# Token gathers of a recommendation kernel: two rows a buffer, a fill after each gather, adds three groups later

## The chip, the cores and the metric

The kernel runs on one core of one Trainium2 chip. The metric is the device time of one execution in microseconds (us), as the median of several executions without a profiler. Before the change it is 5566.13 us, the median of three runs (5557.75, 5566.13 and 5580.29). The engines are named as in the profile: PE is the matrix engine and PEld its weight loads, DVE the vector engine, ACT the scalar engine, POOL the GpSimd engine, SP the sync engine.

## The reference

For 16384 samples, a wide-and-deep recommendation model. Each sample has 32 token indices into a table of 50000 rows of 300 floats, three lists of 20 indices into small tables (1000, 5000 and 10000 rows of 64), and four single indices into tables of 20 to 1000 rows. All is float32.

```python
tok = word_emb[token_idx].mean(axis=1)          # 32 rows of 300 floats
e1 = emb_mh1[mh1_idx].mean(axis=1)              # 20 rows of 64; e2, e3 alike
o1 = emb_oh1[oh1_idx]                           # one row of 64; o2, o3, o4 alike
emb = jnp.concatenate([tok, e1, e2, e3, o1, o2, o3, o4], axis=1)   # 748 wide
...
```

On `emb` follow three layers with bias and relu (748 to 1024 to 512 to 256) and a last one to a single number. A "wide" sum of one weight per small-table index is added to it, and a sigmoid gives the output.

## The kernel before

The 16384 samples are cut into 128 tiles of 128 samples, one sample to a partition; four tiles make a block of 512 samples, on which the three layers run.

The token rows [...] are gathered from HBM: one indirect DMA on POOL (line 188) fetches one row of 300 floats for each of the 128 partitions. A tile needs 32 of them, the whole kernel 4096. The generator `tokens` (line 180) makes them in groups of `TOK_GROUP` = 4 into one buffer of the pool `tokp` (line 81, three buffers), at a pitch of 320 floats after 32 floats of margin. DVE then adds the four rows: two and two at once (line 196, 600 elements), then the two halves (line 204), then into the tile's row `g` (line 205); the first group of a tile adds the halves straight into `g` (line 202). A gather into a buffer must wait until DVE has added up what the buffer held three groups before, and each gather also waits for the gather eight before it to have landed, since eight semaphores take turns.

The small tables are not gathered. For each sample a count of how often each row is used is made by one-hot vectors: `one_hots` (line 252) compares indices with an iota on DVE (line 260), `counts` (line 268) multiplies the one-hots on PE (line 278) and ACT writes the counts to SBUF as 8-bit floats (line 285). `small_sums` (line 293) multiplies the counts with the tables on PE (line 303), and DVE folds the result into `g` (line 310). `transposed` (line 338) turns four finished `g` on PE (line 345) and DVE scales them (line 346); `mlp` (line 365) runs the layers (line 353 on PE, line 362 on ACT).

The order on each engine is the order in which the program is written (`manual_schedule`, line 411). A loop over 128 tiles holds a loop of `STEPS` = 11 steps. In each step the program writes, in this order: the one-hots of the next step, the counts of this step, the due share of `tokens` of this tile, the due share of `small_sums` of the tile before, and the due share of `mlp` of the block before. `Paced` (line 387) decides what is due: in step i it asks for more until done * 11 >= size * i. So DVE meets, in order, the compares of a step, then any token adds of that step, then the compares of the next; an add that waits for a gather holds the compares behind it.

```python
it, ix = load_indices(0)
...
            toks = Paced(tokens(g, it[:, s, :].bitcast(U32)), N_TOK // TOK_GROUP, STEPS)
        for i in range(STEPS):
...
                counts(cnt, hot_now, i)
                toks.go()
```

Of the kernel before, what the change touches and what calls it, by code (L numbers as in the profile page):

```python
# [8 lines left out]
F32 = mybir.dt.float32  # L9
# [8 lines left out]
P = 128  # L18
N_TOK, TOK_D = 32, 300
N_MH, EMB = 20, 64  # L20
ROW = EMB + 1
D1, D2, D3 = 1024, 512, 256
TOK_GROUP = 4
TOK_PITCH = 320
BLOCK = 512
HALF = P // 2
N_SMALL = 3 * N_MH + 4
# [17 lines left out]
def kernel(  # L45
# [21 lines left out]
    nc = tc.nc  # L67
# [7 lines left out]
    for f in SMALL:  # L75
        n = -(-tables[f].shape[0] // P)
# [1 line left out]
        n_h += n  # L78
    PER_BANK = 512 // n_h

    tokp = ctx.enter_context(tc.tile_pool(name="tok", bufs=3))
    const = ctx.enter_context(tc.tile_pool(name="const", bufs=1))
    idxp = ctx.enter_context(tc.tile_pool(name="idx", bufs=2))
    keyp = ctx.enter_context(tc.tile_pool(name="keys", bufs=1))
# [40 lines left out]
    first = const.tile([P, 2, N_SMALL], I32, name="first")  # L125
# [10 lines left out]
    for part0 in range(0, n_h, PART):  # L136
        raw = cp.tile([P, PART, ROW], F32, name="raw", tag="counts")
        for f in SMALL:
            table, (h0, h1) = tables[f], slices[f]
            full, rest = divmod(table.shape[0], P)  # L140
            a, b = max(h0, part0), min(h0 + full, part0 + PART)
            if a < b:
                nc.sync.dma_start(
                    out=raw[:, a - part0 : b - part0, :],
# [5 lines left out]
        for a in range(0, PART, 23):  # L150
            b = min(a + 23, PART)
# [25 lines left out]
    bd_sb = const.tile([1, 1], F32, name="bd_sb")  # L177
    nc.scalar.dma_start(out=bd_sb, in_=bd)

    def tokens(g, it):  # L180

        for q in range(N_TOK // TOK_GROUP):

            space = tokp.tile([P, TOK_GROUP * TOK_PITCH + 64], F32, name="tok_rows")
            rows = space[:, 32 : 32 + TOK_GROUP * TOK_PITCH].rearrange("p (t d) -> p t d", d=TOK_PITCH)
            for t in range(TOK_GROUP):
                j = q * TOK_GROUP + t
                nc.gpsimd.indirect_dma_start(  # L188
                    out=rows[:, t, 0:TOK_D],
                    out_offset=None,  # L190
                    in_=word,
                    in_offset=bass.IndirectOffsetOnAxis(ap=it[:, j : j + 1], axis=0),
                )
            n = TOK_GROUP // 2
            while n > 1:
                nc.vector.tensor_add(  # L196
                    rows[:, 0:n, 0:TOK_D], rows[:, 0:n, 0:TOK_D], rows[:, n : 2 * n, 0:TOK_D]
                )
                n //= 2
            first, second = rows[:, 0, 0:TOK_D], rows[:, 1, 0:TOK_D]  # L200
            if q == 0:
                nc.vector.tensor_add(g[:, 0:TOK_D], first, second)
            else:
                nc.vector.tensor_add(first, first, second)  # L204
                nc.vector.tensor_add(g[:, 0:TOK_D], g[:, 0:TOK_D], first)  # L205
            yield 1

    def load_indices(blk):


        b0 = blk * BLOCK
        it = idxp.tile([P, NSUB, N_TOK], I32, name="it")
        nc.sync.dma_start(
            out=it, in_=idx[b0 : b0 + BLOCK, 0:N_TOK].rearrange("(s p) c -> p s c", p=P)
        )
        ix = keyp.tile([P, NSUB // 2, 2, N_SMALL], I32, name="ix")
        for s in range(NSUB):
            nc.sync.dma_start(
                out=ix[(s % 2) * HALF : (s % 2 + 1) * HALF, s // 2],
                in_=idx[b0 + s * P : b0 + (s + 1) * P, IDX_MH:IDX_COLS].rearrange(  # L220
                    "(f p) c -> p f c", p=HALF
                ),
            )
        return it, ix

    def lookup_keys(ix):

        pairs = NSUB // 2
        low = keyp.tile([P, pairs, 2, N_SMALL], I32, name="low")
        nc.vector.tensor_single_scalar(low, ix, P - 1, op=ALU.bitwise_and)
        nc.vector.tensor_single_scalar(ix, ix, 7, op=ALU.logical_shift_right)
        keys = keyp.tile([P, pairs, 2, 2 * N_SMALL], BF16, name="keys")
        for r in range(pairs):
            view = keys[:, r].rearrange("p w (f c) -> p w f c", f=2)
            nc.vector.tensor_copy(view[:, 0], low[:, r])  # L238
            nc.vector.tensor_add(view[:, 1], ix[:, r], first)
        pk = ps_h.tile([P, pairs, 2, P], BF16, name="pk", tag="ph")  # L240
        for r in range(pairs):
            for w in range(2):
                nc.tensor.transpose(pk[:, r, w, :], keys[:, r, w, :], ident_bf)  # L243
        sc = scp.tile([P, pairs, 2, 2, HALF, 2], BF16, name="sc")
        n = pairs * 2 * P
        nc.vector.tensor_copy(
            sc.rearrange("p r w t b d -> p (r w t b) d"),
            pk.rearrange("p r w b -> p (r w b)").unsqueeze(2).to_broadcast([P, n, 2]),
        )
        return sc  # L250

    def one_hots(sc, s, i):

        b = i * ONEHOT
        rows = min(ONEHOT, HALF - b)
        row1 = ohp.tile([P, ONEHOT, P], BF16, name="row1")
        slice1 = ohp.tile([P, ONEHOT, n_h], BF16, name="slice1")
        for w, (one, n) in enumerate(((row1, P), (slice1, n_h))):
            shape = [P, rows, n // 2, 2]
            nc.vector.tensor_tensor(  # L260
                one[:, 0:rows, :].rearrange("p i (n d) -> p i n d", d=2),
                iota[:, 0:n].rearrange("p (n d) -> p n d", d=2).unsqueeze(1).to_broadcast(shape),
                sc[:, s // 2, w, s % 2, b : b + rows, :].unsqueeze(2).to_broadcast(shape),
                ALU.is_equal,
            )
        return row1, slice1
# [26 lines left out]
    def small_sums(g, cnt):  # L293


        by_slice = cnt.rearrange("l f p h -> l (f p) h")
        for i in (0, 2, 6, 4):
            pair = SMALL[i : i + 2]
            pg = ps_g.tile([P, 2, 3 * ROW], F32, name="pg")
            for j, f in enumerate(pair):  # L300
                h0, h1 = slices[f]
                for h in range(h0, h1):
                    nc.tensor.matmul(  # L303
                        pg[:, j, :], by_slice[:, :, h], terms[:, h, :], start=(h == h0), stop=(h == h1 - 1)
                    )
                    if h < h1 - 1:
                        yield 1
            at = TOK_D + i * ROW
            n = len(pair)
            nc.vector.tensor_reduce(  # L310
                g[:, at : at + n * ROW].rearrange("p (f d) -> p f d", f=n),
                pg[:, 0:n, :].rearrange("p f (c d) -> p f d c", c=3),
                AX.X,
                ALU.add,
            )
            yield n if i != 6 else n + LULL

    def wide_term(g):
        wide = wp.tile([P, 1], F32, name="wide")
        at = TOK_D + EMB  # L320
        nc.vector.tensor_reduce(
            wide,
            g[:, at : at + 6 * ROW].rearrange("p (c d) -> p c d", d=2 * ROW)[:, :, 0:2],
            AX.XY,
            ALU.add,
        )
        nc.vector.tensor_add(wide, wide, g[:, G_COLS - 1 : G_COLS])
        return wide
# [87 lines left out]
    for t in range(tiles + 1):  # L416
        s = t % NSUB
        sums = None
        if before:
            sums = Paced(small_sums(*before), n_h + LULL, STEPS)  # L420
        if t < tiles:
            if s == 0 and t:
                it, sc = next_it, next_sc
            g = gp.tile([P, G_COLS], F32, name="g")
            cnt = cp.tile([P, 2, HALF, n_h], FP8, name="cnt", tag="counts")
            toks = Paced(tokens(g, it[:, s, :].bitcast(U32)), N_TOK // TOK_GROUP, STEPS)
        for i in range(STEPS):
            if t < tiles:
                hot_now = hot
                if s == 1 and i == 0 and t + NSUB < tiles:  # L430
                    next_it, ix = load_indices(t // NSUB + 1)
                if s == 2 and i == 0 and t + NSUB < tiles + 1:
                    next_sc = lookup_keys(ix)
                if i < STEPS - 1:
                    hot = one_hots(sc, s, i + 1)
                elif t + 1 < tiles:
                    hot = one_hots(next_sc if s == NSUB - 1 else sc, (s + 1) % NSUB, 0)
                counts(cnt, hot_now, i)
                toks.go()
            if sums:  # L440
                sums.go()
            if layers:
                layers.go()
        if before:
            sums.finish()
            gs.append(before[0])
            wides.append(wide_term(before[0]))
        before = (g, cnt) if t < tiles else None
        if len(gs) == NSUB:
            if layers:  # L450
                layers.finish()
            layers = Paced(mlp(t // NSUB - 1, transposed(gs), wides), mlp_size, NSUB * STEPS)
            gs, wides = [], []
# [40 lines left out]
```

## Time and profile before

| what | value |
|---|---|
| median of three runs | 5566.13 us |
| the profiled execution's own time | 7340.1 us |
| its span from first to last instruction | 7338.3 us |
| busy: PE, DVE, ACT, POOL | 5808.1, 3542.7, 2657.3, 4082.8 us |
| mean granted clock of PE | 0.889 |
| busy share of the 16 DMA engines by the gathers | 31.9% |

The profiled execution took 7340.1 us, 1774 us more than the median without a profiler. So its durations of single instructions and its order of events are of use, but its idle time is not that of an undisturbed run. "Busy" counts the time in which an instruction of the engine was recorded as running; a wait is idle time, put down to what ended it. "remote" and "another core or an unknown queue" are waits whose end the profile can't give to an instruction, and "issue" is idle time in which the engine waited for nothing that the profile shows. [...]

### The profile page before, as it was taken

The numbers are of one execution on the slowest core, as the hardware profiler recorded it, in microseconds if no ns is written. First come the engines' busy times: TensorE is split into PE (matmuls) and PEld (weight loads), VectorE is DVE, ScalarE is ACT, GpSimd is POOL, SyncE is SP. The second block draws the span as 40 slices with busy tenths as digits, with TensorE's granted clock in tenths as the row PEclk, the third lists the DMA queues.
The fourth block names the chain that finished last, engine by engine and source line by source line (L and its number), as shares of the span: only waits on it lengthen the run. The fifth ranks groups of instructions, "written<-read, shape, count | busy, mean of one in ns | idle before, by whom it ended". The sixth has DMA issues, their size and how long they took to land.

```text
span 7338.3 us, 100239 instructions
## 1 busy us (share of the span) xinstructions
PE 5808.1 (79%) x40960; PEld 3442.6 (47%) x40960; DVE 3542.7 (48%) x6977; ACT 2657.3 (36%) x3383; POOL 4082.8 (56%) x4103
## 2 busy tenths in 40 slices
PE   2688888888778787888878788878877878888789
PEld 2444444444444444444444444444444444444444
DVE  4444445445444454445445445445544444445442
ACT  4333333333333333333333333333333333333332
POOL 5555555555555555555555555555555555555551
PEclk8798888888888888888899998888898989888899
DMA  4333333333333333333333333333333333333330
GB/s 130 94 89 92 88 89 90 91 90 88 88 90 89 88 85 90 89 88 90 93 89 94 90 90 89 91 86 91 88 89 90 88 87 90 93 89 88 86 91 25
DMA packets 242809, 652.34 MB, mean 89 GB/s; under 512 B 105631, under 2 KB 109471, under 8 KB 242347
## 3 DMA queue, kind: packets, MB, share of 16 engines
q0 software_dynamic: 196608, 629.41, 31.9%
q1 hardware_dynamic: 42738, 10.83, 0.8%
q8 instruction: 320, 5.24, 0.3%
q10 hardware_dynamic: 3001, 5.69, 0.2%
q14 instruction: 142, 1.16, 0.1%
HBM read 645.59 MB, written 0.07 MB: 88 GB/s over the span
## 4 chain that ended last, share of the span: by engine, by line
PE 59%; another core or an unknown queue 20%; ACT 10%; issue 7%; DVE 3%; DMA 0%; SPq 0%; DVEq 0%; ACTq 0%
PE ph L353 27%; PE pg L303 21%; PE pc L278 9%; ACT cnt L285 9%; PE pt L345 1%; ACT h L362 1%; DVE x L346 1%; DVE g L310 1%; PE po L375 1%; PE pk L243 0%; PE po L377 0%; DMA raw<-in_mh_dram 0%; DVE slice L260 0%; DVE tok_rows L196 0%
## 5 line engine op out<-in xcount | busy, mean ns | idle before, releaser
L188 POOL DMA_INDIRECT tok_rows<-in_word_emb_dram,it x4096 | 4081.9, 997 | 3120.9 <-DVE g L205 1202.3
L285 ACT ACTIVATE cnt<-pc 128x828 fp8e3<-128x828 f32 (+1 forms) x2816 | 2239.5, 840 | 3521.0 <-remote 1890.0
L303 PE MATMUL pg<-terms,cnt 128*128 128x195 bf16 x17664 | 2142.2, 271 | 372.5 <-issue 308.3
L260 DVE TENSOR_TENSOR row<-iota,sc 128x768 bf16<-128x768 bf16 (+1 forms) x1408 | 765.2, 543 | 2667.3 <-remote 1545.4
L303 PEld LDWEIGHTS <-cnt 128*128 128x128 fp8e3 x17664 | 1748.2, 147 | 629.6 <-issue 485.2
L353 PE MATMUL ph<-x,w_sb 128*128 128x512 f32 (+1 forms) x3072 | 1600.2, 647 | 27.1 <-issue 26.1
L278 PE MATMUL pc<-slice,row 64*128 64x138 bf16 x16384 | 858.3, 231 | 940.4 <-ACT cnt L285 640.7
L278 PEld LDWEIGHTS <-row 64*128 64x128 bf16 x16384 | 558.1, 97 | 2050.2 <-issue 1556.8
L353 PE MATMUL ph<-h,w_sb 128*128 128x512 f32 x2560 | 1341.1, 648 | 26.5 <-issue 24.6
L353 PEld LDWEIGHTS ph<-x,w_sb 128*128 128x128 f32 (+1 forms) x3072 | 579.6, 209 | 502.4 <-issue 489.1
L260 DVE TENSOR_TENSOR slice<-iota,sc 128x828 bf16<-128x828 bf16 (+1 forms) x1408 | 808.7, 574 | 0.0
L196 DVE TENSOR_TENSOR tok_rows<-tok_rows 128x600 f32<-128x600 f32 x1024 | 795.2, 777 | 1.0 <-DMA tok_rows<-in_word_emb_dram,it 0.7
L353 PEld LDWEIGHTS ph<-h,w_sb 128*128 128x128 f32 x2560 | 485.3, 210 | 415.5 <-issue 415.4
L362 ACT ACTIVATE h<-ph,b_sb 128x512 f32<-128x512 f32 x448 | 308.3, 688 | 948.6 <-PE ph L353 495.9
L310 DVE TENSOR_REDUCE g<-pg 128x130 f32<-128x390 f32 (+1 forms) x512 | 251.6, 510 | 787.3 <-remote 286.4
L204 DVE TENSOR_TENSOR tok_rows<-tok_rows 128x300 f32<-128x300 f32 x896 | 423.7, 473 | 30.8
L205 DVE TENSOR_TENSOR g<-g,tok_rows 128x300 f32<-128x300 f32 x896 | 422.0, 471 | 30.7
L346 DVE TENSOR_SCALAR x<-pt,scale 128x512 f32<-128x512 f32 (+1 forms) x192 | 139.6, 749 | 116.1 <-PE pt L345 74.9
L345 PE MATMUL pt<-ident,g 128*128 128x128 f32 (+1 forms) x768 | 132.3, 311 | 71.3 <-DVE x L346 70.3
L345 PEld LDWEIGHTS pt<-ident,g 128*128 128x128 f32 (+1 forms) x768 | 92.6, 154 | 110.0 <-DVE x L346 100.5
L243 PE MATMUL pk<-ident_bf,keys 128*128 128x128 bf16 x128 | 23.7, 241 | 86.7 <-DVE keys L238 85.0
L285 ACT ACT_TABLE_LOAD x31 | 39.8, 1283 | 143.2 <-PE pc L278 143.2
(35 smaller groups left out, 458.7 us busy)
## 6 DMA issues: line engine op xcount, KB each, us to landing
tok_rows<-in_word_emb_dram,it POOLq DMA_INDIRECT x4096
ix<-in_idx_dram SPq DMA_DIRECT2D x128, 32.0 KB
w_sb<-in_W_dram ACTq DMA_DIRECT2D x6, 512.0 KB
w_sb<-in_W_dram ACTq DMA_DIRECT2D x1, 2048.0 KB
it<-in_idx_dram SPq DMA_DIRECT2D x32, 64.0 KB
out_dram<-h SPq DMA_DIRECT2D x32, 2.0 KB
raw<-in_mh_dram SPq DMA_DIRECT2D x1, 422.5 KB
w_sb<-in_W_dram ACTq DMA_DIRECT2D x1, 256.0 KB
```

The source lines that it names most:

```text
L188: nc.gpsimd.indirect_dma_start(out=rows[:, t, 0:TOK_D], out_offset=None, in_=word, in_offset=bass.IndirectOffsetOnAxis(ap=it[:, j : j + 1] ...
L196: nc.vector.tensor_add(rows[:, 0:n, 0:TOK_D], rows[:, 0:n, 0:TOK_D], rows[:, n : 2 * n, 0:TOK_D])
L204: nc.vector.tensor_add(first, first, second)
L205: nc.vector.tensor_add(g[:, 0:TOK_D], g[:, 0:TOK_D], first)
L260: nc.vector.tensor_tensor(one[:, 0:rows, :].rearrange("p i (n d) -> p i n d", d=2), iota[:, 0:n].rearrange("p (n d) -> p n d", d=2).unsque ...
L278: nc.tensor.matmul(pc[:, f, k * n_h : (k + 1) * n_h], hot[0][half, k0 + k, :], hot[1][half, k0 + k, :], start=True, stop=True,)
L285: nc.scalar.activation(cnt[:, :, b + k0 : b + k0 + n, :].rearrange("l f k h -> l f (k h)"), pc[:, :, 0 : n * n_h], AF.Copy, scale=0.5, sat ...
L303: nc.tensor.matmul(pg[:, j, :], by_slice[:, :, h], terms[:, h, :], start=(h == h0), stop=(h == h1 - 1))
L310: nc.vector.tensor_reduce(g[:, at : at + n * ROW].rearrange("p (f d) -> p f d", f=n), pg[:, 0:n, :].rearrange("p f (c d) -> p f d c", c=3) ...
L345: nc.tensor.transpose(pt[:kk, s * P : (s + 1) * P], chunk(g, k), ident)
L353: nc.tensor.matmul(ph, weights[:kk, k, m * P : (m + 1) * P], src[:kk, k, :], start=(k == 0), stop=(k == len(kks) - 1),)
L362: nc.scalar.activation(dst[:, m, :], ph, AF.Relu, bias=bias[:, m : m + 1])
```

## The change

- `TOK_GROUP` goes from 4 to 2. A tile's 32 gathers are now 16 groups of two, and `Paced` asks for one or two groups in each of the 11 steps, where it asked for none or one group of four.
- A buffer holds two rows of 300 floats without margin or pitch, and the pool has six buffers in place of three.
- After each gather, POOL fills a tile `pause` of 128 x 256 floats with zeros. Nothing reads it.
- DVE adds up a group when the third group after it has been issued (`under_way`, `TOK_LAG` = 3); the list runs on from tile to tile, and the last three groups are added by `last_tokens` in the pass after the last tile.
- The sum of a group is one add of two rows and one add into `g`; for a tile's first group it is one add.

```diff
-TOK_GROUP = 4
-TOK_PITCH = 320
+TOK_GROUP = 2
+TOK_LAG = 3
+PAUSE = 256
...
-    tokp = ctx.enter_context(tc.tile_pool(name="tok", bufs=3))
+    tokp = ctx.enter_context(tc.tile_pool(name="tok", bufs=2 * TOK_LAG))
...
+    under_way = []
+    pause = const.tile([P, PAUSE], F32, name="pause")
+
+    def add_up(rows, g, first):
+        a, b, n = rows[:, 0:TOK_D], rows[:, TOK_D : 2 * TOK_D], TOK_D
+        if first:
+            nc.vector.tensor_add(g[:, 0:n], a, b)
+        else:
+            nc.vector.tensor_add(a, a, b)
+            nc.vector.tensor_add(g[:, 0:n], g[:, 0:n], a)
...
         for q in range(N_TOK // TOK_GROUP):
-
-            space = tokp.tile([P, TOK_GROUP * TOK_PITCH + 64], F32, name="tok_rows")
-            rows = space[:, 32 : 32 + TOK_GROUP * TOK_PITCH].rearrange("p (t d) -> p t d", d=TOK_PITCH)
+            rows = tokp.tile([P, TOK_GROUP * TOK_D], F32, name="tok_rows")
             for t in range(TOK_GROUP):
                 j = q * TOK_GROUP + t
                 nc.gpsimd.indirect_dma_start(
-                    out=rows[:, t, 0:TOK_D],
+                    out=rows[:, t * TOK_D : (t + 1) * TOK_D],
...
-            n = TOK_GROUP // 2
-            while n > 1:
-                nc.vector.tensor_add(
-                    rows[:, 0:n, 0:TOK_D], rows[:, 0:n, 0:TOK_D], rows[:, n : 2 * n, 0:TOK_D]
-                )
-                n //= 2
-            first, second = rows[:, 0, 0:TOK_D], rows[:, 1, 0:TOK_D]
-            if q == 0:
-                nc.vector.tensor_add(g[:, 0:TOK_D], first, second)
-            else:
-                nc.vector.tensor_add(first, first, second)
-                nc.vector.tensor_add(g[:, 0:TOK_D], g[:, 0:TOK_D], first)
+                nc.gpsimd.memset(pause, 0.0)
+            under_way.append((rows, g, q))
+            if len(under_way) > TOK_LAG:
+                rows, to, old_q = under_way.pop(0)
+                add_up(rows, to, old_q == 0)
             yield 1
+
+    def last_tokens():
+        for rows, g, q in under_way:
+            add_up(rows, g, q == 0)
...
             toks = Paced(tokens(g, it[:, s, :].bitcast(U32)), N_TOK // TOK_GROUP, STEPS)
+        else:
+            last_tokens()
```

## The prediction

> **What bounds the kernel now.** I read the page's busy table first, then the group of the gathers, then what POOL waited for, and last the order of time on POOL in a stretch of steady work.
>
> The busy table, and the dearest group of the page (line, engine, operation, tiles, count, then busy us and mean ns, then idle us before it and what ended it):
>
> ```profile
> PE 5808.1 (79%) x40960; PEld 3442.6 (47%) x40960; DVE 3542.7 (48%) x6977; ACT 2657.3 (36%) x3383; POOL 4082.8 (56%) x4103
> ...
> L188 POOL DMA_INDIRECT tok_rows<-in_word_emb_dram,it x4096 | 4081.9, 997 | 3120.9 <-DVE g L205 1202.3
> ```
>
> By this table POOL looks half idle. What it waited for (us in total, times, longest):
>
> ```profile
> POOL tok_rows L188 <- DVE g L205: 1202.3, 337, 10.0
> POOL tok_rows L188 <- issue: 1100.2, 3561, 2.4
> POOL tok_rows L188 <- DVE g L202: 753.6, 110, 16.4
> ```
>
> The 1100.2 us of "issue" are 3561 gaps of 0.31 us, one ahead of nearly every gather, for no event. They belong to the gather as much as its 997 ns do. The order of time on POOL (start, us, what, idle before) shows it where nothing else holds POOL:
>
> ```profile
> 3064.43 0.95 POOL L188 DMA_INDIRECT tok_rows<-in_word_emb_dram,it  x1 [0.30 <-issue]
> 3065.68 0.95 POOL L188 DMA_INDIRECT tok_rows<-in_word_emb_dram,it  x1 [0.30 <-issue]
> 3066.94 0.95 POOL L188 DMA_INDIRECT tok_rows<-in_word_emb_dram,it  x1 [0.30 <-issue]
> ```
>
> One gather each 1.25 us; with the mean of 0.997 us in place of 0.95, 1.302 us. All 4096 of them make 4096 x 1.302 = 5333 us. The tile view puts the first at 38.4 us and the last at 7203.3 us of 7338.3, so 38 us lie ahead and 135 us behind: 5333 + 173 = 5506 us as the least time that POOL allows at these durations. The median is 5566.13 us, 60 us more. In the profiled execution (7340.1 us, span 7338.3) POOL has 1202.3 + 753.6 = 1956 us of waiting for DVE to free a buffer; in an execution of 5566 us there is room for almost none. Worked back, (5566 - 173) / 4096 = 1.317 us a gather.
>
> What made DVE late in the profile is this (idle us, times, longest):
>
> ```profile
> ACT cnt L285 <- remote: 1890.0, 485, 13.9
> ...
> DVE row L260 <- remote: 1545.4, 299, 12.9
> ```
>
> Those waits have no releaser in the trace and can't all be there in a run that is 1774 us shorter; I take them as the profiled execution's own. Without them PE is not far from POOL: the first count matmuls of neighbouring steps stand 3.49 us apart in smooth stretches (3034.45, 3037.94, 3041.44). Summing, for each of the 44 steps of a block, the tenth percentile of its length gives 164.2 us, or 41.05 us a tile, against 32 x 1.302 = 41.7 us on POOL. So I read the kernel as bound by the rate of gathers, with PE within 2% of it.
>
> [...] 0.30 us stand ahead of each gather, and still 0.27 us pass between the add that frees its buffer (end 3048.93) and its start (3049.20). [...] The trace has no gather next to a fill. [...] Of the gathers that no DVE operation overlapped, none of 1892 took over 1.05 us; those overlapped by over 1 us took 1.12 us in the mean, so they do contend. [...]
>
> **The change, part by part.**
>
> *The fills.* 4096 more instructions on POOL, in its order after each gather. A fill of 128x256 does not occur before; the nearest rows are fills of one column and of 128 columns, at the start:
>
> ```profile
> 0.33 0.12 POOL L479 MEMSET const-uint8-127<- 128x1 uint8 x1
> 0.74 0.20 POOL masks.py:197 MEMSET ident<- 128x128 f32 x1 [0.29 <-POOLq L479]
> 0.99 0.23 POOL L121 IOTA iota_i<- 128x138 int32 x1
> ```
>
> The float32 fill of one column took 0.105 us in the mean, of 128 columns 0.205 us (group view): 0.79 ns a column, so 0.306 us for 256, an estimate. Bounds: below, 0.205 us, if its start is hidden (the small fills start 0.03 us apart while each lasts 0.1 us); above, 0.306 plus a gap like the gather's, 0.305, so 0.61 us. Below nothing only if the fill lies in the 0.30 us gap. I take 0.306, in series: period 1.302 + 0.306 = 1.608 us, 4096 x 1.608 = 6586 us, + 173 = 6760 us. Its wait on POOL's own semaphore is for the fill before, a whole gather earlier: nothing. Behind the fill stands the next gather.
>
> What covers it? In the profiled execution the 1956 us of waiting for DVE would, and 4096 x 0.306 = 1253 us fit in. There the change would cost about nothing: POOL's sum of 6760 us is below 7338. In the 5566 us of the median there is no such cover, 60 us at most. So I expect the profile to move little and the median to move by 6760 - 5566 = +1194 us, +21%.
>
> *Groups of two.* On DVE a group of four cost 0.777 + 0.473 + 0.471 = 1.72 us, two groups of two cost 2 x (0.473 + 0.471) = 1.89 us. In all: before 795.2 + 423.7 + 422.0 + 60.3 = 1701 us; after 1920 x 0.944 + 128 x 0.471 = 1873 us, +172 us. DVE then has 3715 us in over 5500, and nothing on POOL waits for it if POOL is the last: hidden. If POOL were not, it would be up to 172 us.
>
> *The lag and the six buffers.* 3 x 4 rows and 6 x 2 rows hold the same twelve. A gather waits for the add of the group six before, which is written three groups earlier in the order. An add now waits for data that was due three groups (5 to 8 us) before, so the compares behind it on DVE, and PE behind those, can run up to three groups ahead. That lets PE run more smoothly, but PE is not last once POOL needs 32 x 1.608 = 51.5 us a tile. The three last groups are added after the last tile's gathers: under 3 us in the tail.
>
> *Pitch 1200 instead of 1280 bytes.* The gathers keep the 16 DMA engines busy for 31.9% of 7338 us, 0.57 us of each 1.30 us period. Even a fifth more is hidden. SP, ACT and PE keep their instructions.
>
> *Sum.* 173 + 4096 x (1.302 + 0.306) = 6760 us, DVE's 172 us hidden.
>
> **The rivals.**
>
> 1. The fill pays a gap of its own, as gathers do: 173 + 4096 x (1.302 + 0.306 + 0.305) = 8009 us. For it: the gap stands before every gather. Against: fill and iota at the start are 0.05 us apart. I give the stretch from 7150 to 8010 us to it.
> 2. The fill lies in the gap: [...] POOL stays at 1.31 us a gather: 5570 us. Against: the gap is there with a gather just ended and with POOL long idle alike.
> 3. Faster: outside the profiler a gather takes well below 1.30 us, PE at 41.05 us a tile is the bound, and the loss above it is DVE held by adds that wait for gathers, which the lag of three groups removes. Time: 173 + 128 x 41.05 = 5427 us, -2.5%. It decides at gather plus fill = 41.05 / 32 = 1.283 us; above it POOL is the last again. For it: PE's busy 79% is the highest. Against: a gather never took under 0.943 us, plus 0.305 and the fill's least, 0.205, makes 1.45.
>
> That the change does not do what it says is no rival: the order of POOL's instructions has a fill after each of the 4096 gathers.
>
> **How the numbers follow.** Fill in series 62% (6145 to 7150 us), gap of its own 18% (to 8010), hidden in the gap 8% (5570), faster 12% (5427). The low end of the first is a gather without any DVE contention and the least fill: 173 + 4096 x (0.948 + 0.305 + 0.205) = 6145. The range leaves out the last two, 2 in 10: 6145 to 8010 us. A measurement of this kernel can tell about 0.5% from no change. Slower: 62 + 18 = 80%. Within 0.5% is the hidden fill: 8%. Faster 12%.
>
> **What would show it.** Right: the group of the fill has about 0.3 us each; fill and gather alternate with starts of gathers 1.55 to 1.65 us apart where POOL waits for nothing; POOL's waits for DVE shrink by 1000 us or more, while the profiled span stays near 7340 us. The adds then wait for gathers. Wrong: gathers still 1.25 us apart with a fill between (rival 2), 1.9 us apart (rival 1), or a median under 5540 us with PE's steps at 3.5 us (rival 3). The weakest point is that the rate of gathers is taken from the profile to a run that is a quarter shorter.

## The result, and the profile after

| kernel | median us | range, runs | ratio to before, 95% interval |
|---|---|---|---|
| before | 5566.45 | 5557.75 to 5580.29, 4 | |
| changed | 6366.10 | 6360.32 to 6374.79, 4 | 1.1435 [1.1408, 1.1462] |

The change makes the kernel 14.4% slower: 800 us, where 1194 us were forecast (6760 us; range 6145 to 8010). The profiled execution of the changed kernel took 6374.79 us, as long as its other runs. The profile of the kernel before (7340.1 us) and the experiments e9 to e12, which ran on another chip than e1 to e8, show conditions in which the kernel before takes 7340 to 7710 us, with or without a profiler, while beside all other runs it takes 5550 to 5581 us, so idle time can't be compared across the two.

The page of the changed kernel: busy times, the chain of work that ended last (by engine, then by line), and the groups of the gathers and the fills (busy us, mean ns, idle us before it):

```profile
PE 5411.0 (85%) x40960; PEld 3259.1 (51%) x40960; DVE 3695.0 (58%) x8001; ACT 2637.3 (41%) x3383; POOL 5513.6 (87%) x8199
...
POOL 66%; DMA 12%; issue 9%; DVE 7%; PE 5%; POOLq 0%; ACT 0%; DVEq 0%; SPq 0%; ACTq 0%
...
L199 POOL DMA_INDIRECT tok_rows<-in_word_emb_dram,it x4096 | 4177.4, 1020 | 742.8 <-issue 646.9
...
L205 POOL MEMSET pause<- 128x256 f32 x4096 | 1345.4, 328 | 2.1
```

POOL is now busy for 87%, and the 742.8 us of idle time ahead of the gathers are for the most part "issue", the gaps that go with a gather. The chain that ended last runs over POOL for two thirds of the span. What the engines waited for (us, times, longest) in the changed kernel:

```profile
ACT cnt L293 <- PE pc L286: 2768.2, 1227, 9.4
DVE tok_rows L189 <- DMA tok_rows<-in_word_emb_dram,it: 2301.5, 1659, 4.1
...
POOL tok_rows L199 <- issue: 646.9, 3775, 1.3
```

DVE's adds wait 2301.5 us for gathered rows, and POOL waits for almost nothing. The trace of before has 1956 us of waits for a buffer, and "remote" waits; here are none of either, but as the two profiles were taken in different conditions, the change can't be credited with that. The order of time on POOL and DVE shows the new beat (start, us, what, idle before):

```profile
3005.23 0.95 POOL L199 DMA_INDIRECT tok_rows<-in_word_emb_dram,it  x1 [0.17 <-issue]
...
3006.19 0.33 POOL L205 MEMSET pause<- 128x256 f32 x1
...
3006.68 0.95 POOL L199 DMA_INDIRECT tok_rows<-in_word_emb_dram,it  x1 [0.17 <-issue]
```

The fill begins when the gather has ended, and the next gather begins 0.17 us after the fill, where 0.30 us stood between two gathers before. From gather to gather it is 1.45 us here, and over all of them, from the first start at 39.0 to the last at 6257.7 us, 6218.7 / 4095 = 1.519 us.

### The profile page after: what moved, and what is told of

Its sections match the earlier page's. It is cut to its first block, busy times and chain, and to the rows that moved or that the text cites. A ratio compares the mean times of both kernels' runs of the same rounds, so it can differ in the third digit from the quotient of the medians.

```text
span 6373.0 us, 106380 instructions
## 1 busy us (share of the span) xinstructions
PE 5411.0 (85%) x40960; PEld 3259.1 (51%) x40960; DVE 3695.0 (58%) x8001; ACT 2637.3 (41%) x3383; POOL 5513.6 (87%) x8199
## 4 chain that ended last, share of the span: by engine, by line
POOL 66%; DMA 12%; issue 9%; DVE 7%; PE 5%; POOLq 0%; ACT 0%; DVEq 0%; SPq 0%; ACTq 0%
POOL tok_rows L199 50%; POOL pause L205 16%; DMA tok_rows<-in_word_emb_dram,it 12%; DVE tok_rows L189 2%; PE ph L361 2%; DVE g L190 2%; DVE g L318 1%; PE po L383 1%; DVE row L268 1%; DVE x L354 1%; PE pt L353 1%; PE pg L311 1%; POOLq L199 0%; PE po L385 0%; DVE slice L268 0%
## 5 line engine op out<-in xcount | busy, mean ns | idle before, releaser
L199 POOL DMA_INDIRECT tok_rows<-in_word_emb_dram,it x4096 | 4177.4, 1020 | 742.8 <-issue 646.9
L189 DVE TENSOR_TENSOR tok_rows<-tok_rows 128x300 f32<-128x300 f32 x1920 | 908.5, 473 | 2305.8 <-DMA tok_rows<-in_word_emb_dram,it 2301.5
L311 PE MATMUL pg<-terms,cnt 128*128 128x195 bf16 x17664 | 1927.2, 261 | 243.2 <-DVE g L318 243.2
L311 PEld LDWEIGHTS <-cnt 128*128 128x128 fp8e3 x17664 | 1659.8, 145 | 409.2 <-issue 260.3
L361 PE MATMUL ph<-x,w_sb 128*128 128x512 f32 (+1 forms) x3072 | 1536.1, 627 | 0.0
L205 POOL MEMSET pause<- 128x256 f32 x4096 | 1345.4, 328 | 2.1
L361 PE MATMUL ph<-h,w_sb 128*128 128x512 f32 x2560 | 1290.3, 630 | 0.0
L286 PE MATMUL pc<-slice,row 64*128 64x138 bf16 x16384 | 783.0, 229 | 577.9 <-DVE slice L268 560.2
L190 DVE TENSOR_TENSOR g<-g,tok_rows 128x300 f32<-128x300 f32 x1920 | 905.8, 472 | 65.7
L293 ACT ACT_TABLE_LOAD x31 | 39.8, 1283 | 145.9 <-PE pc L286 116.6
L187 DVE TENSOR_TENSOR g<-tok_rows 128x300 f32<-128x300 f32 x128 | 60.2, 471 | 63.2 <-DMA tok_rows<-in_word_emb_dram,it 63.1
```

The source lines that it names most:

```text
L189: nc.vector.tensor_add(a, a, b)
L190: nc.vector.tensor_add(g[:, 0:n], g[:, 0:n], a)
L199: nc.gpsimd.indirect_dma_start(out=rows[:, t * TOK_D : (t + 1) * TOK_D], out_offset=None, in_=word, in_offset=bass.IndirectOffsetOnAxis(ap ...
L205: nc.gpsimd.memset(pause, 0.0)
L286: nc.tensor.matmul(pc[:, f, k * n_h : (k + 1) * n_h], hot[0][half, k0 + k, :], hot[1][half, k0 + k, :], start=True, stop=True,)
L293: nc.scalar.activation(cnt[:, :, b + k0 : b + k0 + n, :].rearrange("l f k h -> l f (k h)"), pc[:, :, 0 : n * n_h], AF.Copy, scale=0.5, sat ...
```

## The experiments

Theory A is that of the prediction: POOL makes gathers without a break in both kernels, so all that lengthens its period lengthens the run. Rival B: the smaller groups, their extra adds or the lag cost the time. Rival C: PE bounds the kernel before.

### e1: the lag and the groups of two, without the fills

```diff
-                nc.gpsimd.memset(pause, 0.0)
```

> The changed kernel without its fills; groups of two, six buffers and the lag stay. Theory A (POOL's gathers bound both kernels, the fill alone made the change slower): a gather of about 1.02 us and a gap of 0.305 us give 4096 x 1.32 + 155 = about 5570 us, as before (5500 to 5620), and the profile shows starts of gathers 1.25 us apart or a little more. Rival B (the groups of two, the extra DVE adds or the lag cost the time): 6200 us or more. Rival C (a gather takes less outside the profiler, PE bounds the kernel before, and the lag frees DVE): about 5430 us.

Measured: 5528.95 us, ratio 0.9943 [0.9926, 0.9959]. Its profile (5529.1 us span) has no fill and the old gap. The tile view of its gathers (duration ns least/median/most, first and last start):

```profile
L198 POOL DMA_INDIRECT tok_rows<-in_word_emb_dram,it x4096: 942/949/1816, 38.6 to 5414.2; - x196
```

That is (5414.2 - 38.6) / 4095 = 1.313 us a gather. POOL never stops for anything else: of the 4095 gaps between gathers one, at the start, is over 0.4 us. The difference of the periods, 4096 x (1.519 - 1.313) = 844 us, accounts for the difference of the two medians, 6366.1 - 5529.0 = 837 us. So the fill alone costs, and rival B falls: without it the change gains 0.6%.

### e2: the fills in the old order

```diff
-TOK_PITCH = 320
+TOK_PITCH = 304
...
                     in_offset=bass.IndirectOffsetOnAxis(ap=it[:, j : j + 1], axis=0),
                 )
+                nc.gpsimd.memset(pause, 0.0)
```

> The kernel before with a fill of 128x256 after each gather, and a pitch of 304 in place of 320 floats to make room for the fill's tile; groups of four, three buffers, no lag. Theory A: the same POOL period as the changed kernel, 1.52 us, so 6366 us within 60. Rival B: about 5570 us, since the fill is not what costs.

Measured: 6371.79 us, ratio 1.1458 [1.1439, 1.1477]: the time of the changed kernel, with groups of four and no lag. How the gathers are grouped and added up makes no difference once the fill is there.

### e3, e4 and e11: the length of the fill

```diff
-PAUSE = 256
+PAUSE = 1
```

(512 in e4, 128 in e11)

> The changed kernel with a fill of one column instead of 256. Theory A with the gap as measured after the change (0.165 us after a fill instead of 0.305 us after a gather): 1.02 + 0.10 + 0.165 = 1.285 us, 4096 times and 155 us: 5420 us by POOL, and PE's own pace then gives 5430 to 5520 us. If the gap ahead of a gather is a fixed 0.305 us and the short gap after the change had another reason: 1.02 + 0.10 + 0.305 = 1.425 us, 5990 us.

> The changed kernel with a fill of 512 columns instead of 256. Theory A: the fill grows from 0.328 us to 0.328 + 256 x 0.79 ns = 0.53 us, the period from 1.519 to 1.72 us, the time to 155 + 4096 x 1.72 = 7200 us (7100 to 7300), all of the added fill on the path. Rival B: the time stays near 6370 us.

> The changed kernel with a fill of 128 columns. The model from the runs so far: the next gather starts 0.305 us after the last one ended or 0.165 us after the fill ended, whichever is later. A fill of 128 columns takes 0.22 us, so 0.385 us between gathers and 1.01 us a gather: 4096 x 1.395 + 155 = 5870 us (5820 to 5930). If the fill were simply added to the run without fills: 5529 + 4096 x 0.22 = 6430 us. If all of it were hidden up to 0.305 us: 5530 us.

Measured: e3 5572.57 us, ratio 1.0018 [1.0009, 1.0027]; e4 7076.18 us, ratio 1.2727 [1.2706, 1.2748], 24 us under the range that was expected; e11 7225.24 us beside 7632.39 us of the kernel before, far from the 5870 us expected. The order of time on POOL with one column:

```profile
3003.42 0.95 POOL L199 DMA_INDIRECT tok_rows<-in_word_emb_dram,it  x1 [0.19 <-issue]
3004.37 0.11 POOL L205 MEMSET pause<- 128x1 f32 x1
3004.67 0.95 POOL L199 DMA_INDIRECT tok_rows<-in_word_emb_dram,it  x1 [0.19 <-DVE keys L247]
```

and with 512:

```profile
3000.90 0.95 POOL L199 DMA_INDIRECT tok_rows<-in_word_emb_dram,it  x1 [0.16 <-issue]
3001.86 0.54 POOL L205 MEMSET pause<- 128x512 f32 x1
3002.56 0.95 POOL L199 DMA_INDIRECT tok_rows<-in_word_emb_dram,it  x1 [0.17 <-issue]
```

With one column the gathers start 1.25 us apart, as with no fill at all: a fill of 0.118 us and a gap of 0.19 us fill just the 0.305 us that stood there before. With 512 columns a fill of 0.54 us and a gap of 0.165 us make 0.70 us. Median times from the traces:

| columns | fill us | gap after it us | end of gather to next gather us |
|---|---|---|---|
| none | | | 0.305 |
| 1 | 0.118 | 0.191 | 0.305 |
| 128 | 0.219 | 0.165 | 0.384 |
| 256 | 0.326 | 0.165 | 0.491 |
| 512 | 0.540 | 0.165 | 0.704 |

So neither of the expectations for e3 held: the gap is neither fixed after the fill nor 0.165 us whatever the fill. A rule that fits all five rows: the next gather starts 0.305 us after the gather before ended, or some 0.165 us after the fill ended, whichever is later. By this rule some 0.14 us of fill is free, and all beyond it is paid; no fill between 0.118 and 0.219 us was tried, and why part of the gap can run beside a fill is open. In time, e4 less the changed kernel is 710 us, against 4096 x (0.540 - 0.326) = 877 us of added fill; the rest came back since a gather took 0.981 us in the mean instead of 1.020 us. Of the gathers, which stand 1.69 us apart there, 57% overlap a two-input operation (TENSOR_TENSOR) of DVE, against 83% in the changed kernel; e8 shows what such an operation does to a gather.

e3 ran 44 us longer than e1 with the same beat. The trace has 38 gaps of 0.95 to 1.5 us before a gather, with no releaser, 48 us in all, where e1 has none; the changed kernel has 38 too, of 0.5 to 1.3 us. In both they stand after 113 gathers and then after every 106 more, and at just these places the gap in e12 is 0.336 us in place of 0.165; in e2 they come after 113 and then every 212. So they go with a place in POOL's program and not with what DVE or PE do at the time. What they are is open.

For e11 the beat is as the rule says (0.384 us), but its time says nothing of the fill, since POOL waited for DVE there:

```profile
POOL tok_rows L199 <- DVE g L190: 1426.6, 406, 10.0
```

It shows something else: where POOL has time to spare, the kernel with groups of two, the lag and a fill of 128 columns was 5.3% faster than the kernel before beside it (ratio 0.9469 [0.9438, 0.9501]). Which part of the change does that was not tried; by e10 it is not the pitch.

### e5 and e6: PE's pace and POOL's pace by themselves

```diff
-            rows = tokp.tile([P, TOK_GROUP * TOK_D], F32, name="tok_rows")
-            for t in range(TOK_GROUP):
-                j = q * TOK_GROUP + t
-                nc.gpsimd.indirect_dma_start(
...
+            rows = still
```

> The changed kernel without fills and without gathers: DVE adds up, as before, one tile of zeros instead of gathered rows, so the token sums are left out of the output and all other work stays. It gives the pace of PE and DVE alone. Theory A (gathers bound the kernel before and PE is close behind): below 5500 us; by the estimate of 41.05 us a tile 5430 us, or less[...]: 5150 to 5430 us. Theory C (PE bounds the kernel before): 5540 us or more.

```diff
-            under_way.append((rows, g, q))
-            if len(under_way) > TOK_LAG:
...
+            last.append(rows)
+            del last[: -2 * TOK_LAG]
...
-                counts(cnt, hot_now, i)
...
+        for _ in tokens(None, it[:, s, :].bitcast(U32)):
+            pass
```

> The 4096 gathers and the loads of their indices alone, into the same six buffers, with no adds, no counts, no layers and no other work beside them (the output is not computed). It gives POOL's rate outside the profiler with DVE out of the way. Theory A: 0.949 + 0.305 = 1.254 us a gather, as in the profile: 4096 x 1.254 + about 50 = 5190 us (5170 to 5230). If gathers are faster outside the profiler: clearly less, 4900 us or below.

Measured: without gathers 5247.17 us (0.9419 [0.9393, 0.9445] of before), gathers alone 5171.84 us (0.9284 [0.9259, 0.9309]). Without gathers, PE is busy nearly throughout:

```profile
PE 5093.3 (97%) x40960; PEld 3097.0 (59%) x40960; DVE 3659.0 (70%) x8002; ACT 2630.1 (50%) x3383; POOL 0.9 (0%) x7
```

Gathers alone take, in the group view of that kernel (busy us, mean ns, idle before):

```profile
L198 POOL DMA_INDIRECT tok_rows<-in_word_emb_dram,it x4096 | 3876.6, 946 | 1285.2 <-issue 1247.5
```

0.946 us and a gap of 0.305 us, 1.251 us each, with nothing else on the core: 4096 x 1.251 + 46 = 5170 us, the time measured without a profiler. The rows land 1.92 us after the recorded end of their gather (median), so the time on POOL is not that of the transfer. So the rate read from the trace of before holds outside the profiler, and rival C falls: PE without gathers is 5.8% below the kernel before. And neither engine alone makes 5530 us. Of the 357 us between e6 and e1, 4096 x (1.313 - 1.251) = 254 us come from longer gathers, and 108 us from longer ends (154 us in place of 46). The longer gathers are those that meet DVE: in e1 the 471 that no two-input operation of DVE overlapped took 0.947 us, as alone, and all together 1.007 us in the mean.

### e12: gathers and fills alone

The fill is added to the kernel of e6:

```diff
+    pause = const.tile([P, PAUSE], F32, name="pause")
...
                     in_offset=bass.IndirectOffsetOnAxis(ap=it[:, j : j + 1], axis=0),
                 )
+                nc.gpsimd.memset(pause, 0.0)
```

> The 4096 gathers, each with its fill of 256 columns, and nothing else beside them (the output is not computed). Same model, no DVE work to wait for: 0.947 + 0.326 + 0.165 = 1.438 us, 4096 x 1.438 + 46 = 5936 us (5920 to 5950). The difference to the changed kernel, 430 us, is then what DVE's operations add to the gathers, and the tail of 115 us.

Measured: 5983.62 us; 5936 were expected (5920 to 5950), so it is 0.8% over, and outside the range. The gather took 0.956 us in place of the 0.947 expected. The same 4096 fills in the kernel of e6 add 812 us, as in the full kernel (837 us); the two ran on different chips, but almost nothing other than POOL works in either. So the fills cost their time with no other engine beside them. The group view of e12:

```profile
L199 POOL DMA_INDIRECT tok_rows<-in_word_emb_dram,it x4096 | 3915.8, 956 | 718.7 <-issue 680.9
L205 POOL MEMSET pause<- 128x256 f32 x4096 | 1346.3, 329 | 2.3
```

### e7: groups of two, no lag

```diff
-TOK_LAG = 3
+TOK_LAG = 0
...
-                nc.gpsimd.memset(pause, 0.0)
...
-    tokp = ctx.enter_context(tc.tile_pool(name="tok", bufs=2 * TOK_LAG))
+    tokp = ctx.enter_context(tc.tile_pool(name="tok", bufs=6))
```

> The changed kernel without fills and with a lag of 0: groups of two in six buffers, added up in the step that gathers them. It parts the lag from the group size. If the lag brings the gain of 0.6% that the run without fills showed: 5560 us, as before. If the smaller groups bring it: 5530 us. In its profile, waits without a known releaser as in the kernel before (over 1000 us) if it is the lag that removes them, none if it is the group size.

Measured: 5521.31 us, ratio 0.9914 [0.9886, 0.9941]. The lag gives nothing here, where POOL binds; the small gain without fills belongs to the groups of two in six buffers (or to the pitch, see e10). This is the fastest full kernel that was run, 0.9% below the kernel before. Its trace has no waits without a releaser, but by e9 that says nothing of the lag or of the group.

### e8: four rows summed by a reduce

```diff
-        a, b, n = rows[:, 0:TOK_D], rows[:, TOK_D : 2 * TOK_D], TOK_D
+        four = rows.rearrange("p (t d) -> p d t", t=TOK_GROUP)
...
-            nc.vector.tensor_add(a, a, b)
-            nc.vector.tensor_add(g[:, 0:n], g[:, 0:n], a)
+            part = sump.tile([P, TOK_D], F32, name="part")
+            nc.vector.tensor_reduce(part, four, AX.X, ALU.add)
+            nc.vector.tensor_add(g[:, 0:TOK_D], g[:, 0:TOK_D], part)
```

> The changed kernel without fills, with groups of four in three buffers, a lag of one group, and the four rows summed by one reduce of DVE, which has one input in SBUF, and one add into the tile's row. The adds with two SBUF inputs go from 3840 + 128 to 896. Theory A with contention ([...] 1.007 us in the mean instead of 0.949): the added time of a gather falls from 0.058 to about 0.034 us, 4096 x 0.024 = 98 us less than 5529: 5430 us (5400 to 5480), if PE's pace allows. Without that contention: 5529 us or more.

Measured: 5619.05 us, ratio 1.0082 [1.0053, 1.0110]: a miss, slower instead of faster. The contention is there, though. POOL and DVE in order of time in that kernel:

```profile
3003.16 1.27 POOL L200 DMA_INDIRECT tok_rows<-in_word_emb_dram,it  x1 [0.30 <-issue]
3003.54 0.58 DVE L268 TENSOR_TENSOR slice<-iota,sc 128x828 bf16<-128x828 bf16 x1
3004.04 2.23 DVE L190 TENSOR_REDUCE part<-tok_rows 128x300 f32<-128x1200 f32 x1
3004.74 0.94 POOL L200 DMA_INDIRECT tok_rows<-in_word_emb_dram,it  x1 [0.30 <-issue]
3005.99 0.95 POOL L200 DMA_INDIRECT tok_rows<-in_word_emb_dram,it  x1 [0.30 <-issue]
```

The gather that meets the compares takes 1.27 us, those beside the reduce 0.94 us. Over the whole trace, the 1677 gathers that began during a reduce of token rows took 0.946 us in the mean, as if alone, and none over 1.0 us; the 874 that began during a compare (two inputs in SBUF) took 1.18 us. In the changed kernel the 715 gathers that met no two-input operation of DVE took 0.952 us in the mean, none over 0.961, and those that met one 1.034 us. Fills took 0.326 us in the median there with or without DVE beside them. What in such an operation holds up a gather was not shown.

But the gathers gained nothing in the mean (1.006 us): those that began during compares took longer than in e1 (1.18 us, where 807 took 1.11). And for four rows the reduce, which reads 1200 elements at a pitch of 300, took 2.25 us and its add 0.47 us more, against 1.89 us for the adds of two groups of two. DVE, busy 4531 us of 5623, became a second limit:

```profile
L190 DVE TENSOR_REDUCE part<-tok_rows 128x300 f32<-128x1200 f32 x896 | 2016.3, 2250 | 759.6 <-DMA tok_rows<-in_word_emb_dram,it 758.6
...
POOL tok_rows L200 <- DVE part L190: 121.2, 96, 5.3
```

Once in each block of 128 gathers POOL waits 0.8 to 5.3 us until DVE has freed a buffer: 32 waits, 102 us in all, where e8 is 98 us longer than e7.

### e9 and e10: the kernel before once more, and the pitch

> The kernel before, unchanged, profiled once more. It asks whether the long profiled execution (7340 us against a median of 5566 us) comes each time. If it belongs to this kernel under the profiler: again 7000 us or more, with over 1000 us of waits without a known releaser. If it was one odd execution: about 5560 us.

```diff
-TOK_PITCH = 320
+TOK_PITCH = 300
...
-            space = tokp.tile([P, TOK_GROUP * TOK_PITCH + 64], F32, name="tok_rows")
-            rows = space[:, 32 : 32 + TOK_GROUP * TOK_PITCH].rearrange("p (t d) -> p t d", d=TOK_PITCH)
+            space = tokp.tile([P, TOK_GROUP * TOK_PITCH], F32, name="tok_rows")
+            rows = space.rearrange("p (t d) -> p t d", d=TOK_PITCH)
```

> The kernel before with rows at a pitch of 300 floats and without the margin of 32; groups of four, three buffers, no lag, no fills. It takes the last part of the change by itself. If pitch and margin matter to the transfers: 5600 us or more. If they don't (theory A; packets take 0.28 us in the mean with either): 5560 us, and the 0.9% of the run with groups of two comes from the group size.

Measured: e9 7705.8 us, a single profiled run, with the same kind of waits as in the first profile of before:

```profile
ACT cnt L285 <- remote: 1793.1, 506, 12.0
DVE row L260 <- remote: 1676.4, 280, 11.5
```

e9 asked whether the long execution belongs to the profiler. It does not: the kernel before took 7591 to 7695 us in 23 runs beside it without a profiler. It is not one odd execution either. Gathers and fills alone (e12, beside it) ran within 0.8% of their sum, so it is not the gathers that were slow there; the waits stand where ACT and DVE wait for PE. Why the kernel takes longer there was not settled: the chip differed, and no run varied it alone.

e10: 7640.79 us, ratio 1.001 [0.9994, 1.0026]. The pitch makes no difference where POOL has time to spare. Where gathers bind it was not tried by itself; e1 and e7 have the pitch of 300 and lose nothing by it.

## Why the prediction was right, and where it was not

**POOL is the bound, though its page shows 56%.** Held. Gathers alone take 5172 us, all other work without them 5247 us, together 5529 to 5566 us; so PE is close behind, but in e1 POOL doesn't wait after its start, and 154 us at the ends and 4096 periods of 1.313 us make 5532 us, its time but for rounding. Of the kernel before there is no trace in the conditions of its median; with the same ends its 5562 us beside e1 leave 1.320 us a gather, which is some 31 us more in all than in e1. Adding the gap to the busy time of the gather gave it: a third of what looked idle (1100 of 3121 us) was part of the gather.

**The fill in series, +0.306 us a gather.** The place and the sign held; this term was mis-sized. The fill took 0.328 us in the mean, more than the estimate. But the prediction kept the gather's gap of 0.305 us behind it ("period 1.302 + 0.306"), and it shrank to 0.172 us in the mean. Net: 0.328 - 0.134 + 0.013 for a slightly longer gather = 0.207 us, 848 us in place of 1253. That the time lies in the range owes something to luck: the low end kept the 0.305 us too, and took 0.510 us for gap and least fill, where 0.500 us were measured. The low end (6145 us) was worked out for gathers that DVE does not hold up; such gathers took 5984 us with their fills in e12, or 6111 us with the 173 us of the forecast at the ends in place of 46. Rival 2 was thus right for the first 0.14 us of a fill, and rival 1 not at all (the fill starts within 0.01 us of the gather's end). The evidence given against rival 2, that the gap is there after an idle POOL too, did not exclude that part of it runs beside a fill.

**PE within 2% of POOL.** Too near: PE's pace without gathers is (5247 - 154) / 128 = 39.8 us a tile, not 41.05. The 41.05 came from a trace with 0.889 of PE's clock granted; e5 has 0.998. That this is why it was too long is likely, but no run shows it. In four traces, PE busy for 79, 85, 93 and 97% of the span goes with 0.889, 0.941, 0.985 and 0.998 of the clock (before, changed, e1, e5); which follows from which they don't show. Nothing in the forecast of 6760 us hung on it.

**Groups of two, +172 us on DVE, hidden.** Held: the adds of token rows take 1874.5 us (1873 forecast), DVE's busy time rose from 3542.7 to 3695.0 us in all, and e1 is not slower for it.

**The lag lets PE run ahead, without worth.** Held where POOL binds: by e7 against e1 without fills, by e2 against the changed kernel with them. Rival 3, in which the lag wins because gathers are faster outside the profiler, falls with that and with e6. Where POOL does not bind, e11 leaves open whether the lag helps.

**"Those waits ... I take them as the profiled execution's own", and so a profiled span near 7340 us.** Wrong. The kernel before takes 7591 to 7695 us without a profiler too, on another chip (e9), and the changed kernel's profile came out at its median. The forecast of the median did not suffer, since it was built from the period of POOL and not from idle time.

**Signs.** Starts 1.55 to 1.65 us apart were announced; they are 1.445 us where DVE is out of the way and 1.519 us in the mean. Fills of about 0.3 us and adds waiting for gathers were found. POOL's waits for buffers are gone as announced, but e1 has none after its start without a fill either, and e11 has 1426.6 us of them with one: they go with the conditions of the run.

## What to carry to other kernels

For an engine that issues gathers, take the time from one start to the next in a stretch where nothing holds it, times the count, and compare that with the run: the busy share misses the gap between instructions, here 0.305 us beside each 0.946 us of a gather alone (e6). An instruction put in "to spread work out" on such an engine is free only up to the part of that gap that can run beside it, here some 0.14 us, and it must be tried with the engine's own free-running rate in mind, not with the idle time of a trace whose total is far above the median. What such an instruction costs depends on which engine binds: e11, with a fill of 128 columns, was 5.3% faster than the kernel before where POOL had time to spare. And measure the two candidates for the bound alone: two cut-down kernels settled here what the waits in the trace could not.

## What the runs showed of the hardware that was not expected

- A gather of 128 rows of 1200 bytes costs POOL 0.946 us and 0.305 us until the next can start, 1.251 us, with nothing else on the core.
- A fill between two gathers is free for about 0.14 us (an estimate, 0.305 - 0.165 from the gaps); the rest is paid: 0.384, 0.491 and 0.704 us from the end of a gather to the next with fills of 0.219, 0.326 and 0.540 us. A fill of c columns of float32 took about 0.11 us + c x 0.84 ns (0.118, 0.219, 0.326 and 0.540 us for 1, 128, 256 and 512).
- A gather that meets a two-input operation of DVE takes longer: in the mean 1.034 us, against 0.952 us for those that met none (changed kernel). In e8 those that began during a compare took 1.18 us in the mean, and those that began during the reduce of token rows 0.946 us, as alone.
- DVE's reduce over four rows, read at a pitch of 300 floats, took 2.25 us for 1200 elements in e8, 1.9 ns each; the add of two rows 1.57 ns for each of its 300 results.
